# A region-attention and depthwise-convolution kernel: the convolution of image 2 in two halves, its steps and image 1's spread over bands 19 to 32, and the projection to 256 channels spread over three regions

## The chip, the cores and the metric

The kernel runs on one core of one Trainium2 chip. A core has five engines that run their own instruction streams in program order: TensorE (matmul, PE in the profile, with PEld for its weight loads), VectorE (DVE), ScalarE (ACT), GpSimdE (POOL) and SyncE (SP), which here only issues DMAs. The metric is the time of the device in microseconds, and the median of three runs stands for the kernel before.

## The reference

The input is four images of 128 channels and 128 x 128 pixels. The first layer takes from each image 9 x 9 overlapping regions of 16 x 16 pixels (step 14) and does in each a LayerNorm over channels, attention with four heads of 32, a projection and a residual; overlapping pixels are averaged. Then comes a LayerNorm over channels, a projection from 128 to 256 channels, a depthwise 5 x 5 convolution, a batch norm with the statistics of all four images, two GELUs, a projection back to 128 and a residual:

```
out = zeros.at[:, :, ih, iw].add(reg2);  merged = out / cnt
y  = ln(merged^T) @ w_p0 + b_p0                      # 128 -> 256 channels
ym = conv(ym, dw_k, padding 2, feature_group_count=256)   # depthwise 5x5
ym = batchnorm over (batch, rows, columns) of ym
y  = gelu(gelu(ym)) @ w_p2 + b_p2 + merged
```

The second layer quantises activations and weights and does two 3 x 3 convolutions with batch norms and a residual. The change doesn't touch it.

## The kernel before, in words

The first layer runs in 36 bands (`bands`, t = 0 to 35): band t is row i = t mod 9 of regions of image t // 9, with 9 regions side by side. All engines but POOL run in the order in which the program lists the work (`tc.manual_schedule`). The loop over t goes through the nine regions j of a band; for each it issues `scores(j)` (L784, with the exponentials L792 on ACT), then the pending `values` of the region before (L847, L855, and on DVE L867 to L871), and between these four lists of side work that `beside(t)` has planned for region j.

The side work of band t is the LayerNorm and the q/k projections of band t+1 (`ln1_chunks`, two blocks of rows a1 and a2), the output projection, second LayerNorm and projection to 256 of band t-1 (`post_chunks`, blocks b1 and b2), and steps of the depthwise convolution of rows that are complete. The last four entries of a block, b1[7:] and b2[7:], are its projection to 256, called `p0` (L561): four matmuls `pm<-xn,wp` (eight PE instructions, L438), one ACT instruction into a tile `y` (L567), and a store of that tile to the scratch tensor `y2_d`. There are four `y` tiles, two for each half of the 256 channels (L204), taken in turn. So a `p0` must wait until the store of the tile two before in its half has landed. In bands from 10 on, b1's four `p0` run in region 8 and b2's four in region 0 of the next band (`left`, L922); in bands up to 9 they are spread over three regions (L939).

The depthwise convolution is done on TensorE with band matrices. `units` (L170) lists its portions: images 0 to 2 each as a whole (8 groups of 16 rows), image 3 as 4, 2 and 2 groups. `conv_steps(n)` (L615) makes a portion's steps: the first only loads two tiles ahead, each of the rest loads the tile two ahead (`w<-dw_d` L587, `u<-y_d` L634) and does the `products` of one: matmuls L601 into two PSUM tiles `pm`, two ACT copies `c` (L648), bn_stats on DVE (L652) and stores of the copies to `cv_d`. A whole image has 32 such tiles of 2 x 4 channels by 8 groups (48 instructions on PE with 512 columns, four u loads, two w loads for every second tile, two stores of 256 KB). A half of an image has 16 tiles of 2 x 8 channels by 4 groups (96 instructions with 256 columns, four u loads, two w loads, four stores of 128 KB). The copies lie in the pool `cp`, two buffers each of c0 and c1, so four. There are three `pm` buffers in PSUM, which all side work shares, and three buffers each for u and w. The last portion, two groups, is done after the bands by `conv_rest` (L679, copies L721).

Stores are not issued where they arise: `run` (L944) issues on SP, after each piece of side work, the stores that were pending before it. SP has one queue in program order, and each DMA waits there for what it needs; the DMAs use eight semaphores in turn, and a new DMA on a semaphore waits until the one before it on the same semaphore is complete.

How many steps a band gets is set in `beside` by `todo` and `share`: a whole image's 33 steps are dealt over nine bands (3 or 4 a band: bands 10 to 18 and 19 to 27), image 2's over five (L893: 6 or 7 a band, bands 28 to 32), image 3's first half in bands 33 and 34 (8 and 9), its next portion in band 35 (17). Up to nine steps go to regions in the order of the tuple (1, 3, 5, 7, 8, 4, 6, 2, 0): four steps to regions 1, 3, 5, 7, a fifth to region 8, seven to 1, 3, 4, 5, 6, 7, 8. In odd regions a step is in the second list, in even ones at the end of the fourth.

After the bands come `conv_rest`, the batch norm's constants, `gelu_stage` and `last_stages`.

Of the kernel before, what the change touches and what calls it, by code (L numbers as in the profile page):

```python
# [8 lines left out]
F32 = mybir.dt.float32  # L9
# [5 lines left out]
P = 128  # L15
# [4 lines left out]
NR = (P - RS) // STEP + 1  # L20
# [11 lines left out]
GR = 16  # L32
CW = P // 2
KD = 2 * (GR + 4)
NCK = 8
# [11 lines left out]
def layers(  # L47
# [30 lines left out]
    B = x.shape[0]  # L78
# [45 lines left out]
    g1, b1 = vector(ln1_g, "g1"), vector(ln1_b, "b1")  # L124
# [3 lines left out]
    g2, b2 = vector(ln2_g, "g2"), vector(ln2_b, "b2")  # L128
# [7 lines left out]
    with (  # L136
# [21 lines left out]
        for w in (wqkv, wp0.rearrange("p h m -> p (h m)")):  # L158
            n = w.shape[1]
# [8 lines left out]
    bands = [(b, i) for b in range(B) for i in range(NR)]  # L168

    units = [(b, 0, P // GR) for b in range(B - 1)] + [(B - 1, g, n) for g, n in ((0, 4), (4, 2), (6, 2))]  # L170

# [13 lines left out]
    with ExitStack() as actx:  # L185
# [12 lines left out]
        pool = lambda name, bufs: bctx.enter_context(tc.tile_pool(name=f"{name}_{tag}", bufs=bufs))  # L198
        xp, yp, sums = pool("xp", 2), pool("yp", 2), pool("sums", 1)
        up, cp = pool("up", 3), pool("cp", 2)  # L200
        att, attn_t, attn_v = pool("att", 2 if safe else 4), pool("attn_t", 2), pool("attn_v", 2)
# [413 lines left out]
        def conv_steps(n, ahead=2):  # L615
# [6 lines left out]
            nj = nc_ // 4  # L622
# [18 lines left out]
            def products(at):  # L641
# [4 lines left out]
                for half in range(2):  # L646
                    cv = cp.tile([P, nj, ng, CW], F32, name=f"c{half}")
                    nc.scalar.copy(  # L648
# [30 lines left out]
        def conv_rest(n, w_t, u_t, c_t):  # L679
# [32 lines left out]
            def step(k):  # L712
# [168 lines left out]
        def beside(t, sel=None):  # L881
# [5 lines left out]
            two = post_chunks(t - 1, sel) if t else []  # L887
            had = len(todo)
            if t >= 2:
                b, i = bands[t - 2]  # L890
                if i == NR - 1 and b < B - 1:
                    todo.extend(conv_steps(b))
                    share[0] = NR if b < B - 2 else 5  # L893
                elif b == B - 1 and i == 4:
                    todo.extend(conv_steps(B - 1))
                    share[0] = 2
                elif b == B - 1 and i == 6:
                    todo.extend(conv_steps(B))
                    share[0] = 1

            fresh = len(todo) > had
            n = len(todo) // share[0] if fresh else -(-len(todo) // max(share[0], 1))
            conv = [todo.pop(0) for _ in range(n)]
            share[0] -= 1
            a1, a2 = one if one else ([None] * 9,) * 2
# [9 lines left out]
            d = [[] for _ in range(NR)]  # L915
            twice = len(conv) > NR
# [34 lines left out]
        T = len(bands)  # L951
        todo, share, left, early = [], [0], [], []
        wq, kscale = [], []
# [3 lines left out]
        todo += band_matrices()  # L957
        share[0] = NR + 1
        for blk in row_blocks(0):
# [447 lines left out]
```

## Time and profile before

| What | Value |
|---|---|
| median of 3 runs | 3240.15 us (3233.6 to 3244.1) |
| profiled execution | 3249.98 us, span 3248.2 us |
| PE busy | 3059.6 us, 94% of the span |
| DVE, ACT, POOL busy | 62%, 61%, 26% |
| DMA | 681.70 MB, mean 210 GB/s |
| bands 19 to 32 (1022.5 to 1913.9) | 891.4 us, PE 848.8 us busy, DMA share 0.86 |
| bands 33, 34, 35 | 82.6, 98.3, 104.8 us |

A band starts where its first exponential (L792) starts; there are 18 in each band. In the windows below, each line gives a stretch, its length, each engine's busy time with its instruction count, the granted clock of TensorE, the share of time that the 16 DMA engines were busy, and GB/s. The count on PE tells how many convolution steps a band had: a band without any has 736 (two records are missing in the one shown), each tile of a whole image adds 48, each tile of a half 96. Busy time of PE is modelled, so that a busy PE may be one that waits inside a matmul group.

### The profile page before, as it was taken

The numbers are of one execution on the slowest core, as the hardware profiler recorded it, in microseconds if no ns is written. First come the engines' busy times: TensorE is split into PE (matmuls) and PEld (weight loads), VectorE is DVE, ScalarE is ACT, GpSimd is POOL, SyncE is SP. The second block draws the span as 40 slices with busy tenths as digits, with TensorE's granted clock in tenths as the row PEclk, the third lists the DMA queues.
The fourth block names the chain that finished last, engine by engine and source line by source line (L and its number), as shares of the span: only waits on it lengthen the run. The fifth ranks groups of instructions, "written<-read, shape, count | busy, mean of one in ns | idle before, by whom it ended". The sixth has DMA issues, their size and how long they took to land.

```text
span 3248.2 us, 92154 instructions
## 1 busy us (share of the span) xinstructions
PE 3059.6 (94%) x39162; PEld 1480.1 (46%) x39162; DVE 2014.5 (62%) x3244; ACT 1988.5 (61%) x2658; POOL 840.9 (26%) x1058
## 2 busy tenths in 40 slices
PE   7999999999999999999888998876899999999998
PEld 4555544444444444444344444453544444444443
DVE  5777886766766777676555664542455555666543
ACT  5777777777776777677555655432477777433443
POOL 3444443333333333333222232211111111000000
PEclk9999999999999999999999998876799999999999
DMA  3555677888886888886898988857899999452398
GB/s 82 151 167 162 176 186 191 203 199 204 215 193 169 191 206 211 196 213 172 179 202 201 209 188 203 196 158 187 264 354 359 358 359 304 162 167 80 110 357 311
DMA packets 809891, 681.70 MB, mean 210 GB/s; under 512 B 580918, under 2 KB 695935, under 8 KB 809471
## 3 DMA queue, kind: packets, MB, share of 16 engines
q1 hardware_dynamic: 798879, 669.17, 75.8%
q8 instruction: 311, 5.10, 0.7%
q0 software_dynamic: 1024, 3.93, 0.5%
q10 hardware_dynamic: 9568, 2.61, 0.3%
q14 instruction: 109, 0.89, 0.1%
HBM read 408.72 MB, written 270.79 MB: 209 GB/s over the span
## 4 chain that ended last, share of the span: by engine, by line
PE 76%; DMA 9%; ACT 5%; issue 4%; SPq 3%; DVE 2%; ACTq 0%; POOL 0%; DVEq 0%; POOLq 0%
PE pc L1164 21%; PE pm L438 16%; PE sc L784 9%; PE pm L601 9%; PE po L847 8%; PE pb L1228 6%; PE po L855 3%; DMA y_d<-y 3%; PE pm L377 3%; ACT pt L792 2%; DMA u<-y_d 2%; DMA xn<-row 1%; SPq L451 1%; SPq L431 1%; ACT v L775 1%
## 5 line engine op out<-in xcount | busy, mean ns | idle before, releaser
L867 DVE RECIPROCAL rd<-po 128x256 f32<-128x256 f32 x324 | 568.8, 1756 | 439.1 <-PE po L855 438.5
L1164 PE MATMUL pc<-q,wq 128*128 128x512 fp8e4 x3168 | 700.3, 381 | 5.1 <-DVE q L1176 5.1
L792 ACT ACTIVATE pt<-sc 128x1024 f32<-128x1024 f32 x648 | 628.2, 1025 | 119.1 <-PE sc L784 63.2
L802 POOL TENSOR_TENSOR sm<-pt 128x512 f32<-128x512 f32 x324 | 415.7, 1283 | 1047.3 <-ACT pt L792 727.0
L1164 PEld LDWEIGHTS <-wq 128*128 128x128 fp8e4 x3168 | 309.0, 98 | 406.7 <-issue 38.9
L784 PE MATMUL sc<-q,kr 32*128 32x256 f32 x5184 | 413.6, 417 | 27.3 <-ACT pt L792 27.1
L601 PE MATMUL pm<-u,w 40*32 40x504 f32 (+5 forms) x7680 | 369.6, 503 | 41.7 <-DMA u<-y_d 29.7
L784 PEld LDWEIGHTS sc<-q,kr 32*128 32x128 f32 x5184 | 254.1, 191 | 286.4 <-issue 177.1
L847 PE MATMUL po<-pt,v 128*32 128x256 f32 x5184 | 364.9, 401 | 10.0 <-DVE part L871 6.9
L648 ACT COPY c<-pm 128x512 f32<-128x512 f32 (+1 forms) x256 | 132.4, 563 | 272.3 <-PE pm L601 243.3
L438 PE MATMUL pm<-xn,wp 128*32 128x512 f32 (+1 forms) x2304 | 248.1, 553 | 44.6 <-ACT y L567 42.6
L567 ACT ACTIVATE y<-pm,vectors 128x512 f32<-128x512 f32 (+1 forms) x288 | 183.1, 641 | 166.0 <-DMA y_d<-y 111.9
L802 DVE TENSOR_TENSOR sm<-pt 128x512 f32<-128x512 f32 x324 | 244.2, 754 | 35.8 <-ACT pt L792 35.8
L438 PE MATMUL pm<-xn,wqkv 128*32 128x512 f32 (+1 forms) x2304 | 245.3, 548 | 4.9 <-ACT v L775 3.5
L601 PEld LDWEIGHTS pm<-u,w 40*32 40x32 f32 x7680 | 147.6, 112 | 223.1 <-issue 153.0
L652 DVE BATCH_NORM_STATS2 st<-c 128x6 f32<-128x512 f32 (+2 forms) x320 | 160.9, 550 | 134.8 <-ACT c L648 134.3
L1228 PE MATMUL pb<-cv,wp 128*128 128x512 f32 x512 | 232.1, 596 | 4.9 <-ACT cv L1219 4.9
L847 PEld LDWEIGHTS po<-pt,v 128*32 128x32 f32 x5184 | 140.5, 112 | 186.5 <-issue 103.5
L1172 DVE BATCH_NORM_STATS2 st<-pc 128x6 f32<-128x512 f32 x256 | 165.7, 689 | 84.7 <-PE pc L1164 84.7
L855 PE MATMUL po<-sm,ones 128*32 128x256 f32 x2592 | 206.1, 389 | 0.0
L874 POOL TENSOR_TENSOR ob<-ob,part 128x32 f32<-128x32 f32 x288 | 127.2, 442 | 230.6 <-DVE part L871 224.8
L438 PE MATMUL pm<-wqkv,yr 128*32 128x128 f32 x5184 | 176.3, 273 | 1.2 <-issue 1.2
(157 smaller groups left out, 3394.2 us busy)
## 6 DMA issues: line engine op xcount, KB each, us to landing
cv<-cv_d SPq DMA_DIRECT2D x64, 1024.0 KB
u<-y_d SPq DMA_DIRECT2D x234, 256.0 KB
cv_d<-c SPq DMA_DIRECT2D x192, 256.0 KB
y_d<-y SPq DMA_DIRECT2D x160, 256.0 KB
xn<-row SPq DMA_DIRECT2D x76, 512.0 KB
xfl<-xf_d SPq DMA_DIRECT2D x64, 512.0 KB
id_d<-y SPq DMA_DIRECT2D x64, 512.0 KB
idt<-id_d SPq DMA_DIRECT2D x64, 512.0 KB
```

The source lines that it names most:

```text
L438: nc.tensor.matmul(out[m], w[:, m], v, start=True, stop=True)
L567: nc.scalar.activation(y[:, :n], pm[:, : n * P].rearrange("p (r c e) -> p r e c", r=n, e=2), AF.Identity, bias=bp0[:, h : h + 1],)
L601: nc.tensor.matmul(outs[half][32 * q : 32 * q + 32, j, :, a:z], wt[hs, s, c, :], ut[hs, :, c, a + s - 1 : z + s - 1], start=(s == 1), stop ...
L784: nc.tensor.matmul(sc[h // 2][:, h % 2, kc, :].rearrange("p (r c) -> p r c", c=RS), region(kr, j)[hs, kc * P : (kc + 1) * P], queries(j, h ...
L792: nc.scalar.activation(pt, sc[p], AF.Exp)
L802: add(sm, pt[:, :, 0, :], pt[:, :, 1, :], ALU.add)
L847: nc.tensor.matmul(po[hs, 0, :], v[:, kc, hs], pt[h // 2][:, h % 2, kc, :], start=(kc == 0), stop=(kc == 1),)
L855: nc.tensor.matmul(po[hs, 1, :], ones, sm[h // 2][:, h % 2, :], start=True, stop=True)
L867: nc.vector.reciprocal(rd, po[:, 1, :])
L1164: nc.tensor.matmul(pc[:, h], w[:, t, :], q1[b][:, r + dy : r + dy + RB, dx : dx + P], start=(t == 0), stop=(t == 8),)
L1172: nc.vector.bn_stats(st[:, 2 * n + h, :], pc[:, h])
L1228: nc.tensor.matmul(pb[:, m], wp2[:, h, :], cv[:, h, px], start=(h == 0), stop=(h == 1))
```

## The change

Image 2's convolution is listed in two portions of four groups (64 rows), as image 3's first is, so there are seven portions in place of six. A portion's steps are put on the list when the rows that it needs are complete, at the bands in `ready`. The number of steps in a band now follows one line: 33 over bands 10 to 18, then the 67 of image 1 and of both halves of image 2 over bands 19 to 32, which gives 4, 5, 5, 5, 4, 5, 5, 5, 5, 4, 5, 5, 5, 5. Bands 33 to 35 keep 8, 9 and 17.

In bands 10 to 31 the projection to 256 is split: b1's first two `p0` stay in region 8, its last two move to region 0 of the next band, where one of b2's follows, and b2's last three go to region 2. In a band at which a portion becomes ready all six that are left over stay in region 0.

The copies `c` share three buffers in place of four, in `conv_steps` and in `conv_rest`. The tile of statistics has seven entries per channel group in place of six.

```diff
-    units = [(b, 0, P // GR) for b in range(B - 1)] + [(B - 1, g, n) for g, n in ((0, 4), (4, 2), (6, 2))]
+    units = [(b, 0, P // GR) for b in range(B - 2)]
+    units += [(b, g, n) for b, g, n in ((B - 2, 0, 4), (B - 2, 4, 4), (B - 1, 0, 4), (B - 1, 4, 2), (B - 1, 6, 2))]
...
-        up, cp = pool("up", 3), pool("cp", 2)
+        up, cp = pool("up", 3), pool("cp", 3)
...
-                    cv = cp.tile([P, nj, ng, CW], F32, name=f"c{half}")
+                    cv = cp.tile([P, nj, ng, CW], F32, name="c")
...
-                    cv = c_t.tile([P, 4, ng, CW], F32, name=f"c{half}")
+                    cv = c_t.tile([P, 4, ng, CW], F32, name="c", bufs=3)
...
-                if i == NR - 1 and b < B - 1:
-                    todo.extend(conv_steps(b))
-                    share[0] = NR if b < B - 2 else 5
...
+                if (b, i) in ready:
+                    todo.extend(conv_steps(ready[b, i]))
+            last = T - NR + 6
+            if t <= NR:
+                n = -(-len(todo) // (NR + 1 - t))
+            elif t < last:
+                whole, at = 4 * NCK + 1, t - NR
+                due = whole * at // NR if at <= NR else whole + (2 * whole + 1) * (at - NR) // (last - 2 * NR - 1)
+                n = min(len(todo), due - taken[0])
+                taken[0] += n
+            else:
+                n = len(todo) // 2 if t == last else len(todo)
...
-                d[j] = [conv.pop(0)] if twice and j and conv else []
+                d[j] = [conv.pop(0)] if j and len(conv) > NR - 1 - j else []
...
-            f, left[:] = list(left), b2[7:]
+            apart = t + 1 < last
+            f, left[:] = list(left), [*(b1[9:] if apart else []), *b2[7:]]
+            g = len(f) if t >= 2 and bands[t - 2] in ready else 3
...
-                ([a1[1]], [], f, [*c[0], a1[2]]),
+                ([a1[1]], [], f[:g], [*c[0], a1[2]]),
...
-                ([a2[1]], [a1[4]], b1[:2], [*c[2], a2[2]]),
+                ([a2[1]], [a1[4]], [*f[g:], *b1[:2]], [*c[2], a2[2]]),
...
-                ([], [b2[6], x2], b1[7:], [*c[8], s1]),
+                ([], [b2[6], x2], b1[7 : 9 if apart else None], [*c[8], s1]),
...
+        ends = [(b, NR - 1) for b in range(B - 2)] + [(B - 2, 4), (B - 2, NR - 1), (B - 1, 4), (B - 1, 6)]
+        ready = {at: n for n, at in enumerate(ends)}
```

More of the change, by code (lines that the diff above doesn't have):

```diff
@@ L887, in beside @@
             two = post_chunks(t - 1, sel) if t else []
-            had = len(todo)
             if t >= 2:
                 b, i = bands[t - 2]
-                if i == NR - 1 and b < B - 1:
-                    todo.extend(conv_steps(b))
-                    share[0] = NR if b < B - 2 else 5
[L894 to L902, printed above, removed]
+                if (b, i) in ready:
[10 more added lines that the diff above has]
+                n = len(todo) // 2 if t == last else len(todo)
             conv = [todo.pop(0) for _ in range(n)]
-            share[0] -= 1
             a1, a2 = one if one else ([None] * 9,) * 2
@@ L915, in beside @@
             d = [[] for _ in range(NR)]
-            twice = len(conv) > NR
             for j in sorted((1, 3, 5, 7, 8, 4, 6, 2, 0)[: len(conv)]):
                 c[j] = [conv.pop(0)]
-                d[j] = [conv.pop(0)] if twice and j and conv else []
+                d[j] = [conv.pop(0)] if j and len(conv) > NR - 1 - j else []
             x1 = lambda: fetch(t, 0)
             x2 = lambda: fetch(t, 1)
-            f, left[:] = list(left), b2[7:]
+            apart = t + 1 < last
+            f, left[:] = list(left), [*(b1[9:] if apart else []), *b2[7:]]
+            g = len(f) if t >= 2 and bands[t - 2] in ready else 3
             s1 = early[0][0] if early else None
             plan = [
-                ([a1[1]], [], f, [*c[0], a1[2]]),
+                ([a1[1]], [], f[:g], [*c[0], a1[2]]),
                 ([], [a1[3], *c[1]], [], [a2[0]]),
-                ([a2[1]], [a1[4]], b1[:2], [*c[2], a2[2]]),
+                ([a2[1]], [a1[4]], [*f[g:], *b1[:2]], [*c[2], a2[2]]),
                 ([], [a2[3], *c[3]], [], [b1[2]]),
@@ L951, in layers @@
         T = len(bands)
-        todo, share, left, early = [], [0], [], []
+        todo, left, early, taken = [], [], [], [0]
+        ends = [(b, NR - 1) for b in range(B - 2)] + [(B - 2, 4), (B - 2, NR - 1), (B - 1, 4), (B - 1, 6)]
+        ready = {at: n for n, at in enumerate(ends)}
         wq, kscale = [], []
@@ L957, in layers @@
         todo += band_matrices()
-        share[0] = NR + 1
         for blk in row_blocks(0):
```

## The prediction

> **What bounds the kernel now.** I read the page first (PE is busy 94% of the span, so a gain must come from where PE waits or runs at half clock), then a table of bands, then the waits and the timeline where bands are long.
>
> ```profile
> PE 3059.6 (94%) x39162; PEld 1480.1 (46%) x39162; DVE 2014.5 (62%) x3244; ACT 1988.5 (61%) x2658; POOL 840.9 (26%) x1058
> PEclk9999999999999999999999998876799999999999
> ```
>
> Windows of bands 12, 14, 18, 28, 29, 35, and of the stretch of bands 19 to 32:
>
> ```profile
> 622.10:678.50 56.40, 56.25 (x928) 26.56 (x923) 40.69 (x63) 41.44 (x64) 21.18 (x27) 1.00 0.90 209
> 736.30:794.30 58.00, 56.17 (x928) 26.50 (x920) 40.69 (x63) 41.42 (x64) 21.17 (x27) 1.00 0.87 205
> 966.90:1022.50 55.60, 54.65 (x880) 26.03 (x872) 39.73 (x61) 40.84 (x63) 21.11 (x27) 1.00 0.63 163
> 1540.20:1608.60 68.40, 65.01 (x984) 29.71 (x976) 40.54 (x65) 43.47 (x67) 19.90 (x25) 0.95 0.80 173
> 1608.60:1688.00 79.40, 71.21 (x1072) 32.43 (x1068) 45.38 (x71) 44.74 (x71) 21.12 (x27) 0.94 0.92 201
> 2094.80:2199.60 104.80, 79.09 (x1960) 49.84 (x1957) 43.90 (x106) 37.43 (x66) 17.30 (x20) 0.79 0.63 166
> 1022.50:1913.90 891.40, 848.80 (x13280) 395.85 (x13272) 578.48 (x898) 591.73 (x899) 292.27 (x371) 0.97 0.86 197
> ```
>
> Four tiles (x928) take 56.4 to 58.0 us, three 55.6, seven (x1072) 79.4. So a tile costs some 1 to 2 us up to the fourth and over 7 us beyond it. The first of three reasons is in the timeline of ACT and PE at band 29:
>
> ```profile
> 1597.56 1.07 ACT L648 COPY c<-pm 128x512 f32<-128x512 f32 x2 [1.36 <-PE pm L601]
> 1606.65 1.07 ACT L648 COPY c<-pm 128x512 f32<-128x512 f32 x2 [2.00 <-PE pm L601]
> 1618.03 0.58 ACT L567 ACTIVATE y<-pm,vectors 128x384 f32<-128x384 f32 x1 [4.94 <-DMA y_d<-y]
> 1626.06 0.58 ACT L567 ACTIVATE y<-pm,vectors 128x384 f32<-128x384 f32 x1 [5.68 <-DMA y_d<-y]
> ...
> 1618.66 1.20 PE L438 MATMUL pm<-xn,wp 128*32 128x384 f32 x8 [4.02 <-ACT y L567]
> 1629.17 2.99 PE L784 MATMUL sc<-q,kr 32*128 32x256 f32 x16 [2.87 <-ACT pt L792]
> ```
>
> ACT stands in p0 until the y stores of region 8 land, and PE behind it. After such a stall the granted clock is 0.5 for 3.4 to 6.8 us. In bands 29 to 32 ACT waits 45.2 us for these stores (waits of 1608 to 1914), in bands 12 to 18 13.8. Second, the DMA engines: share 0.92 in band 29. Third, SP, from 28 on: the stores of the copies at 1597.56 are issued only at
>
> ```profile
> 1604.66 2.50 SPq L431 DMA_DIRECT2D cv_d<-c  x2
> 1607.21 4.91 SPq L451 DMA_DIRECT2D xr<-in_x_dram  x1
> 1612.21 4.55 SPq L431 DMA_DIRECT2D y_d<-y  x3
> ```
>
> **The change part by part.** The sum is made against the profiled execution, 3249.98 us, 9.8 (0.3%) above the median; 9.7 us is also about what a measurement can tell from no change.
>
> *Tiles on PE.* The unstalled groups cost the same in both forms, 48 instructions of 512 columns and 96 of 256:
>
> ```profile
> 1623.53 2.78 PE L601 MATMUL pm<-u,w 40*32 40x512 f32 x48
> ...
> 1976.42 2.89 PE L601 MATMUL pm<-u,w 40*32 40x256 f32 x96
> ```
>
> (others of x96 take 2.72 from start to the next instruction). So halving image 2 costs PE nothing; bounds 0 and 32 x 0.11 = 3.5 us. *TensorE: Matmul & The Clock Gate*, section "Wait — 56ns, not 53.3ns?", gives a fixed 2.5 ns for every matmul, which speaks against 1536 more instructions; by it the estimate would be 3.8 us more, where the row says 0 to 3.5.
>
> *DMAs of image 2.* A tile of a half issues ten DMAs (4 u, 2 w, 4 stores) for seven: 32 x 3 = 96 more on SP, at some 0.4 to 0.6 us each 40 to 58 us of SP, which in bands 20 to 26 issues for 24 to 34 of 57 us. The moved steps issue nothing on POOL or ACT, so SP is the only queue that they are moved past. Engine time, from the packets of the trace: u packets of 2048 B at 142 ns in band 34 (320 a tile, 45 us) for 1024 B at 79 ns (640, 51 us); w 120 packets more at 75 ns (9 us); stores of 256 B packets the same. Together +3 us over 16 engines is 0.25 a tile, 8 us for 32.
>
> *Bands 19 to 32.* Tiles per band become 3, 5, 5, 5, 4, 5, 5, 4, 5, 4, 4, 5, 5, 5 (begin steps at 19, 26, 29). Four tiles: 57.3, the mean of such bands. Five: band 28 had five in 68.4 us; 3.3 us of PE idle (waiting for u of the rows just stored, and exp) and half of 6.8 us at clock 0.5 belong to its begin, which leaves 61.7. Lower bound 56.4 + 2.8 = 59.2, if PE alone counts; upper 57.3 + (78.2 - 57.3) / 3 = 64.3, on the line to the seven-tile bands (mean of 29 to 31). I take 61.7, a band of just this load. Band 19: 60.2 and one tile, 61.7. Six p0 in region 0 at bands 24 and 28: +1.5 each (band 10 has six and waits 1.9 us for y). At 29 the begin step falls into region 7 and its first tile into region 8, some 6.5 us later, where SP needs 3.2 us to issue its six loads and u takes 6.3 to land: +6 with the half clock (2 to 10). Begin at 26: +1. Sum 9 x 61.7 + 4 x 57.3 + 61.7 + 3 + 6 + 1 = 856 for 891.4: **-35**. Cross-check by DMA: the share 0.855 of 891.4 is 762 us of engines, with 8 more 770; over 856 a share of 0.90. The highest share in any band is 0.92, which sets the floor at 837 (-54; the GELU stage, 2317 to 2690 us, reaches 0.99, so it is not a hard one); at the old share the stretch takes 900 (+9).
>
> What goes with a stall here: once y is on time, u and the c stores are late next, since DMA stays full. b1's xn is held one region longer; its buffer is wanted by a2's xn load in region 3, two regions later: nothing, and if p0 were that late, SP would stop at L411. DVE gets 64 more bn_stats (128 x 413 ns for 64 x 684: +9.1 us) where it is busy 45 of 79: nothing.
>
> *p0 split, bands 11 to 18.* Clean 56.2, mean of the four-tile bands 57.1; half a dozen such: **-5** (0 to -8).
>
> *Three c buffers.* The second copy of a tile now waits until the first store of the tile before has landed. With two regions between tiles, it would have had 0.4 us or more left in bands 11 to 26 (store landings by the semaphore records): nothing. From region 7 to 8 it has not: copies 9.1 us apart (the rows above), 1.8 less by two p0 fewer, 0.5 more for the second, against a landing 8.0 to 9.1 us after the first copy's end (0.5 later): a wait of 1 to 2 us on ACT. Behind it stand the squares L371 and the next band's exp; PE reaches the sum of squares 0.7 us after them. So some 0.8 us in nine bands: **+7** (0 to 14). In bands 33 and 34 tiles lie one region apart. There the second copies come 0.1 to 9 us too early, 60 us summed over 13; since a wait also puts the next tile later, about half, 30, stays. Most of it is SP being behind, and waiting longer for a store does not make SP later, since loads of u wait for products, not for copies: **+10** (0 to 30). In band 35, likewise 62 us, half 31; but SP issues 161 DMAs for 88.7 of 104.8 us, it sets the pace:
>
> ```profile
> 2137.75 4.83 SPq L431 DMA_DIRECT2D cv_d<-c  x8
> 2142.68 1.58 SPq L587 DMA_DIRECT2D w<-dw_d  x2
> 2144.30 1.57 SPq L634 DMA_DIRECT2D u<-y_d  x4
> 2145.97 3.03 SPq L431 DMA_DIRECT2D cv_d<-c  x4
> ```
>
> so **+4** (0 to 31). In `conv_rest` the second copies have 2.0 to 4.6 us left: 0. The aggregates (64 x 265 ns) grow by a sixth, the last eight are bare: +0.4. One p0 moved at band 34 and a shorter queue at 33: -1.
>
> Sum: -35 - 5 + 7 + 10 + 4 + 0.4 - 1 = -20, so 3230 on the profile's scale and **3220** by the median.
>
> **Rivals.** (A) Slower: the wait for the c stores passes in full to PE in bands 33 to 35, where exp is queued behind the copies and PSUM has three `pm`: 30 + 31 + 14 - 35 - 5 = +35, 3275. It turns the sign when more than 1.0 us of wait per tile reaches PE in these 32 tiles (35 + 5 - 7 = 33). For it: slots that already wait for stores (8.3 us, L648, in band 35). Against it: PE is idle 25.7 of 104.8 us there, mostly for u. (B) The DMA engines were the bound all along, and spreading keeps the share at some 0.875: the stretch takes 880, -11, and -5 + 21 leaves +5: no change, 3245. For it: 0.90 and 0.92 in 12 and 29. Against: band 18 with 0.63, band 28 with 0.80, room that spreading fills. (C) Better: five tiles cost what PE asks and the copies are covered: -54 - 5 + 3 = -56, 3184. For it: band 12 held 0.90 of DMA with PE idle 0.15 us. That the steps don't move can't be: the order is written out.
>
> **How the numbers follow.** Forecast 0.42 (range 3203 to 3234), C 0.2, B 0.19, A 0.19. Faster: 0.4 of the forecast's 0.42, and C: 0.60. Same: most of B and the rest: 0.19. Slower: A and a little of B: 0.21. The range leaves out the far ends of C and A: 3182 to 3262.
>
> **What would show it.** Right: bands 20 to 31 at 57 to 62 us with x928 and x976 (x1216 for five tiles of a half), ACT waiting under 20 us for y stores from band 11 to 32, clock 1.0 there but at 19 and 29; DMA share near 0.90. Wrong: ACT L648 waiting for cv_d stores over 20 us, bands 33 to 35 together over 310 us (285.7 before), five-tile bands at 64 or more.

## The result, and the profile after

The changed kernel takes 3257.8 us in the median of seven runs (3242.0 to 3263.1), where the kernel before takes 3238.7 beside it: ratio 1.005, 95% interval 1.003 to 1.0071. It is slower by half a per cent; the prediction said faster by 0.6%, to 3220. The profiled execution took 3261.4 us, 11.4 more than that of before, where the sum had -20. (Line numbers after the change are one higher than before: the copies are L649, the p0 matmuls L439, the projection's ACT instruction L568.)

The page of the changed kernel, busy times and granted clock, then the groups that the prediction spoke of:

```profile
PE 3064.1 (94%) x40698; PEld 1511.7 (46%) x40698; DVE 2023.7 (62%) x3308; ACT 1984.7 (61%) x2658; POOL 838.8 (26%) x1058
...
PEclk9999999999999999999998988977699999999999
...
L649 ACT COPY c<-pm 128x512 f32<-128x512 f32 (+1 forms) x256 | 135.2, 562 | 360.9 <-PE pm L602 241.7
...
L439 PE MATMUL pm<-xn,wp 128*32 128x512 f32 (+1 forms) x2304 | 256.7, 566 | 16.1 <-ACT y L568 9.0
...
L568 ACT ACTIVATE y<-pm,vectors 128x512 f32<-128x512 f32 (+1 forms) x288 | 182.7, 642 | 99.5 <-PE pm L439 55.6
```

The stalls that the change was priced by did go: PE's wait for `y` is 9.0 us, and the stores of `y` no longer head the list of what ACT waits for before a `y`. The time is elsewhere. Windows of the changed kernel: bands 20, 21, 22, 25 (five whole tiles each), 26 (four tiles of a half and a begin step), 29, 30, 31 (five tiles of a half in the last two), 35; then bands 19 to 25, 26 to 32, 19 to 32 and 33 to 35. (Start and end, length, busy time with count of PE, PEld, DVE, ACT, POOL, granted clock, share of the DMA engines, GB/s.)

```profile
1080.10:1146.80 66.70, 63.73 (x995) 29.49 (x984) 42.57 (x67) 42.44 (x66) 21.10 (x27) 0.95 0.87 196
1146.80:1209.40 62.60, 59.93 (x968) 27.33 (x968) 41.63 (x66) 42.47 (x66) 21.08 (x27) 1.00 0.93 207
1209.40:1273.50 64.10, 59.48 (x968) 27.49 (x968) 41.73 (x66) 42.45 (x66) 21.05 (x27) 0.99 0.93 206
...
1393.70:1452.20 58.50, 58.02 (x956) 26.89 (x960) 41.22 (x65) 42.14 (x66) 20.04 (x24) 1.00 0.94 216
1452.20:1521.80 69.60, 63.16 (x1132) 32.59 (x1124) 42.16 (x72) 42.63 (x65) 21.43 (x27) 0.95 0.80 188
1652.30:1719.60 67.30, 61.71 (x1112) 32.68 (x1104) 41.47 (x72) 41.51 (x65) 21.03 (x27) 0.93 0.77 184
1719.60:1789.30 69.70, 62.91 (x1240) 33.91 (x1234) 43.00 (x76) 42.41 (x65) 21.03 (x27) 0.97 0.79 191
1789.30:1859.20 69.90, 64.80 (x1208) 34.66 (x1208) 42.52 (x76) 42.42 (x66) 21.09 (x27) 0.93 0.82 197
2110.30:2217.50 107.20, 82.31 (x2056) 50.83 (x2048) 44.62 (x106) 37.64 (x67) 17.23 (x20) 0.79 0.66 175
1022.30:1452.20 429.90, 415.36 (x6645) 192.55 (x6640) 288.99 (x450) 294.47 (x450) 145.12 (x184) 0.98 0.90 205
1452.20:1929.30 477.10, 441.32 (x8168) 234.23 (x8160) 294.79 (x513) 297.89 (x453) 146.34 (x187) 0.94 0.82 196
1022.30:1929.30 907.00, 856.68 (x14805) 426.79 (x14796) 583.77 (x963) 592.35 (x902) 291.47 (x371) 0.96 0.86 200
...
1929.30:2217.50 288.20, 234.94 (x5052) 135.53 (x5052) 138.14 (x278) 128.01 (x209) 58.15 (x71) 0.87 0.76 184
```

Set against the sum of the prediction, on the scale of the two profiled executions:

| stretch | before | predicted | measured |
|---|---|---|---|
| bands 0 to 9 | 506.2 | 506.2 | 505.2 |
| bands 10 to 18 (first steps of the split) | 516.3 | 511.3 | 517.0 |
| bands 19 to 25: 32 whole tiles | 405.7 | 429.0 | 429.9 |
| bands 26 to 32: 32 tiles of a half | 485.7 | 427.2 | 477.1 |
| bands 33 to 35 | 285.7 | 299 | 288.2 |
| after band 35 | 1048.6 | 1049 | 1041.6 |

(The two rows in the middle are the prediction's band prices taken apart: 6 x 61.7 + 57.3 + 1.5, and 4 x 61.7 + 3 x 57.3 + 1.5 + 6 + 1. The 7 us of the prediction for waits between regions 7 and 8 are left out here; they lie in nine of the bands 19 to 32.) One row is wrong by 50 us. Of the others, bands 10 to 18 miss the forecast by 6 us, and bands 33 to 35 and the part after band 35 came out 11 and 7 us under it; these partly make up for the 50. Bands of five whole tiles cost what was said, 62.8 us in the mean against 61.7. Bands of five tiles of a half, 27 and 30 to 32, take 69.5. Yet their DMA engines have a share of 0.79 to 0.86, less than the 0.93 of the shorter bands 21 and 22: in the mean of the 16, the engines are less busy there, not more. PE's own work grew little; it waits more, in short pieces, and runs at 0.90 to 0.98 of its clock after them.

The other thing that stands out is what ACT and PE wait for. The view of waits of the changed kernel, ACT's copies and then PE (us in total, times, longest):

```profile
ACT c L649 <- DMA cv_d<-c: 113.4, 36, 7.2
...
PE pm L378 <- ACT sq L372: 48.4, 28, 5.1
PE pm L602 <- DMA u<-y_d: 25.6, 14, 5.9
PE sc L785 <- ACT pt L793: 17.7, 32, 2.1
PE pm L439 <- ACT y L568: 9.0, 2, 8.5
```

and the same of PE in the kernel before:

```profile
PE pm L438 <- ACT y L567: 42.6, 14, 13.6
PE pm L601 <- DMA u<-y_d: 29.7, 18, 6.3
...
PE pm L377 <- ACT sq L371: 7.1, 13, 2.0
```

What PE waited for `y`, it now waits for the squares `sq`, which stand on ACT behind a copy that waits for a buffer. The timeline of band 30 shows one such place:

```profile
1782.63 0.58 ACT L649 COPY c<-pm 128x512 f32<-128x512 f32 x1 [2.02 <-PE pm L602]
...
1787.88 0.58 ACT L649 COPY c<-pm 128x512 f32<-128x512 f32 x1 [4.66 <-DMA cv_d<-c]
1788.36 1.06 ACT L372 ACTIVATE sq<-xt 128x1024 f32<-128x1024 f32 x1
...
1789.47 1.08 PE L378 MATMUL pm<-sq,ones 128*32 128x256 f32 x8 [2.53 <-ACT sq L372]
```

That is the chain of rival A, and it would have been easy to stop here and blame the third buffer. The first experiments ask whether it is the cause.

### The profile page after: what moved, and what is told of

It reads as the page before. It is cut to its first block, busy times and chain, and to the rows that moved or that the text cites. A ratio compares the mean times of both kernels' runs of the same rounds, so it can differ in the third digit from the quotient of the medians.

```text
span 3259.1 us, 95441 instructions
## 1 busy us (share of the span) xinstructions
PE 3064.1 (94%) x40698; PEld 1511.7 (46%) x40698; DVE 2023.7 (62%) x3308; ACT 1984.7 (61%) x2658; POOL 838.8 (26%) x1058
## 3 DMA queue, kind: packets, MB, share of 16 engines
q0 software_dynamic: 1024, 3.93, 0.4%
## 4 chain that ended last, share of the span: by engine, by line
PE 74%; DMA 11%; ACT 5%; issue 4%; DVE 3%; SPq 3%; ACTq 0%; POOL 0%; DVEq 0%; POOLq 0%
PE pc L1165 21%; PE pm L439 16%; PE sc L785 8%; PE pm L602 8%; PE po L848 8%; PE pb L1229 7%; PE po L856 3%; PE pm L378 3%; DMA cv_d<-c 3%; ACT pt L793 2%; DMA u<-y_d 2%; DMA row<-rstd 2%; DMA y_d<-y 1%; DMA xr<-in_x_dram 1%; DVE rd L868 1%
## 5 line engine op out<-in xcount | busy, mean ns | idle before, releaser
L793 ACT ACTIVATE pt<-sc 128x1024 f32<-128x1024 f32 x648 | 627.9, 1024 | 125.0 <-PE sc L785 70.9
L785 PE MATMUL sc<-q,kr 32*128 32x256 f32 x5184 | 405.1, 411 | 20.9 <-ACT pt L793 17.7
L602 PE MATMUL pm<-u,w 40*32 40x252 f32 (+5 forms) x9216 | 367.6, 444 | 39.9 <-DMA u<-y_d 25.6
L649 ACT COPY c<-pm 128x512 f32<-128x512 f32 (+1 forms) x256 | 135.2, 562 | 360.9 <-PE pm L602 241.7
L653 DVE BATCH_NORM_STATS2 st<-c 128x6 f32<-128x256 f32 (+2 forms) x384 | 167.6, 484 | 217.9 <-ACT c L649 217.6
L439 PE MATMUL pm<-xn,wp 128*32 128x512 f32 (+1 forms) x2304 | 256.7, 566 | 16.1 <-ACT y L568 9.0
L602 PEld LDWEIGHTS pm<-u,w 40*32 40x32 f32 x9216 | 173.4, 110 | 207.7 <-issue 129.7
L439 PE MATMUL pm<-xn,wqkv 128*32 128x512 f32 (+1 forms) x2304 | 246.8, 551 | 6.3 <-ACT v L776 4.4
L568 ACT ACTIVATE y<-pm,vectors 128x512 f32<-128x512 f32 (+1 forms) x288 | 182.7, 642 | 99.5 <-PE pm L439 55.6
L439 PE MATMUL pm<-wqkv,yr 128*32 128x128 f32 x5184 | 184.8, 283 | 0.0
```

Of the source, the lines that this page charges most:

```text
L439: nc.tensor.matmul(out[m], w[:, m], v, start=True, stop=True)
L568: nc.scalar.activation(y[:, :n], pm[:, : n * P].rearrange("p (r c e) -> p r e c", r=n, e=2), AF.Identity, bias=bp0[:, h : h + 1],)
L602: nc.tensor.matmul(outs[half][32 * q : 32 * q + 32, j, :, a:z], wt[hs, s, c, :], ut[hs, :, c, a + s - 1 : z + s - 1], start=(s == 1), stop ...
L653: nc.vector.bn_stats(st0[:, k, half, 2 * jj + c0 // 4 + j, n, :], cv[:, j].rearrange("p g x -> p (g x)"))
L785: nc.tensor.matmul(sc[h // 2][:, h % 2, kc, :].rearrange("p (r c) -> p r c", c=RS), region(kr, j)[hs, kc * P : (kc + 1) * P], queries(j, h ...
L793: nc.scalar.activation(pt, sc[p], AF.Exp)
```

## Experiments on the waits for copies

Each kernel ran beside the kernel before on the same chip, which took 3251.5, 3239.1, 3250.6 and 3252.2 us beside the four sets of runs below. So across sets ratios are compared; they are to the kernel before, with 95% intervals. First the changed kernel with four copy buffers. To make room, the statistics of the last portion are put into a small tile late, after band 35 (estimated at about 3 us).

```diff
-        up, cp = pool("up", 3), pool("cp", 3)
+        up, cp = pool("up", 3), pool("cp", 4)
...
-                    cv = c_t.tile([P, 4, ng, CW], F32, name="c", bufs=3)
+                    cv = c_t.tile([P, 4, ng, CW], F32, name="c", bufs=4)
```

> The changed kernel with four c buffers in place of three; the statistics of the last portion lie in a small tile of conv_rest, so that the fourth buffer finds room. Theory W (the copies wait for the stores of the tile before): ACT's waits for cv_d stores fall from 113 us to under 20, bands 19 to 32 from 907 to 855-875 us, bands 33 to 35 from 288 to 280-288, and the median to 3200-3220. Theory H (tiles of a half cost more by themselves, by ten DMAs on SP in place of seven): bands 26 to 32 stay at 465-477 us and the median at 3240-3260. Theory S (the DMA engines are full, whatever the buffers): bands 19 to 32 stay at 890-907 us with a DMA share that does not rise over 0.87.

Measured: 3287.1 us, ratio 1.012 (1.0104 to 1.0137). The waits for copies are all but gone, and the kernel is slower than the changed one. The view of waits of this kernel:

```profile
ACT y L568 <- DMA y_d<-y: 88.6, 43, 16.2
...
ACT c L649 <- DMA cv_d<-c: 10.7, 4, 3.7
```

The waits for stores of `y`, 38.5 us in the changed kernel, are back at 88.6. Its bands 19 to 25 took 430.0 us and 26 to 32 488.6, so bands 19 to 32 and the total are above what any of the three theories had given. Of the 20 us between the two profiled executions 11 lie after band 35 (1053.0 us, where the changed kernel took 1041.6 and the kernel before 1048.6). So that a fourth buffer makes the bands slower is not shown; that it does not cure them is.

The counterpart: the kernel before with three copy buffers and nothing else.

```diff
-        up, cp = pool("up", 3), pool("cp", 2)
+        up, cp = pool("up", 3), pool("cp", 3)
...
-                    cv = cp.tile([P, nj, ng, CW], F32, name=f"c{half}")
+                    cv = cp.tile([P, nj, ng, CW], F32, name="c")
```

> The kernel before with three c buffers, nothing else changed. Theory W: ACT waits 60-120 us for cv_d stores, most of it in bands 28 to 35 where tiles lie one region apart; the median is 20-45 us above the kernel before. Theories H and S: within 10 us of the kernel before.

Measured: 3244.6 us, ratio 0.9979 (0.9965 to 0.9993), a little faster than with four. The view of waits of this kernel, ACT and PE:

```profile
ACT c L648 <- DMA cv_d<-c: 117.3, 41, 7.0
...
ACT y L567 <- DMA y_d<-y: 65.9, 55, 8.5
...
PE pm L377 <- ACT sq L371: 41.1, 24, 6.0
...
PE pm L438 <- ACT y L567: 17.9, 11, 7.4
PE pm L601 <- DMA u<-y_d: 13.6, 9, 3.6
```

ACT waits as long for copies here as in the changed kernel, PE nearly as long for `sq` (41.1 us, there 48.4), and the kernel is not slower, where theory W had wanted 20 to 45 us more: PE's waits for `y` and for `u` fall by as much (42.6 and 29.7 to 17.9 and 13.6). The two runs agree from both sides: having three buffers in place of four moves waits from `y` and `u` to `c`, and it doesn't lengthen the kernel.

## Experiments on the parts of the change

The projection split alone, in the kernel before:

```diff
-                ([a1[1]], [], f, [*c[0], a1[2]]),
+                ([a1[1]], [], f[:g], [*c[0], a1[2]]),
...
-                ([a2[1]], [a1[4]], b1[:2], [*c[2], a2[2]]),
+                ([a2[1]], [a1[4]], [*f[g:], *b1[:2]], [*c[2], a2[2]]),
```

> The kernel before with the projection to 256 spread over three regions in bands 10 to 31, nothing else changed. If y stores hold ACT in the kernel before: ACT's wait for y stores falls from 112 to 30-60 us, bands 29 to 32 from 305 to 285-297 us, and the median by 10-25 us. If other waits take their place: within 8 us of the kernel before.

Measured: 3233.0 us, ratio 0.9947 (0.9929 to 0.9965), a gain of 17 us, within the forecast. Where it arises is another matter. Bands 10 to 18 took 510.5 us (-6) and 19 to 25 396.0 (-10), but bands 29 to 32, which were to fall to 285 to 297 us, took 307.0 (305.4 before), and ACT still waits 66.5 us for stores of `y`, over the 30 to 60 expected. So this part of the change gains, but not in the bands from whose stalls the gain was argued.

The other part alone: image 2 in halves, dealt over bands 28 to 32 as before, four copy buffers (and the late statistics):

```diff
-                    todo.extend(conv_steps(b))
+                    todo.extend(conv_steps(b) if b < B - 2 else conv_steps(b) + conv_steps(b + 1))
```

> The kernel before with image 2 in two halves, dealt over the same bands 28 to 32, with four c buffers (the statistics of the last portion in a small tile of conv_rest). Theory H: bands 28 to 32 grow from 374 to 400-425 us and the median by 25-50 us. Theory W: bands 28 to 32 stay within 10 us of 374, the median within 12 us of the kernel before.

Measured: 3276.0 us, ratio 1.0088 (1.0071 to 1.0105). Bands 28 to 32 went from 373.7 to 393.6 us, between the ranges of the two theories; some 4 us more lie after band 35, with the late statistics. The halves alone lose what the whole change loses and more. So the next question was what in the form of a half tile costs.

## Experiments on the price of a half tile

Against a whole tile, a tile of a half has matmuls of 256 columns, four stores instead of two, and its own load of `w`, where two whole tiles share one. Each was put by itself on the whole tiles of the kernel before. Matmuls of images 0 to 2 in two runs of 256 columns:

```diff
-            for j in range(n // 4):
+            ng = ut.shape[1]
+            for j, g in [(j, g) for j in range(n // 4) for g in range(0, ng, 4)]:
+                gs = slice(g, min(g + 4, ng))
```

> The kernel before with the convolution matmuls of images 0 to 2 done in two runs of 256 columns in place of one of 512, as in the tiles of a half; loads, copies and stores as before. Theory P (the 96 smaller matmuls of a half's tile make it dearer inside a band, although an unstalled group takes the same 2.7 us): 0.6 to 1.5 us for each of 96 tiles, the median 50-140 us above the kernel before. Theories D and B: within 10 us.

Measured: 3245.8 us, ratio 1.0029 (1.0011 to 1.0046), 6.7 us in the median for 96 tiles, 0.07 a tile, inside the bounds 0 to 0.11 of the prediction. That is 1.5 ns for each of 4608 more instructions. By the 2.5 ns that the Trainium skill, *TensorE: Matmul & The Clock Gate*, section "Wait — 56ns, not 53.3ns?", gives for a matmul at the full clock, an estimate would be 11.5 us, which the interval (3.6 to 14.9) does not exclude.

The copies of whole images stored by two DMAs of 128 KB each:

```diff
-                        store(
-                            bass.AP(
+                        for g in range(0, ng, 4):
+                            m = min(4, ng - g)
+                            store(
+                                bass.AP(
```

> The kernel before with each copy of images 0 to 2 stored by two DMAs of 128 KB in place of one of 256 KB: the same bytes in the same 256-byte pieces, two DMAs more per tile, 192 in all. Theory D (the number of DMAs sets the pace, by SP's issue time and by eight in flight): 0.4 to 1 us per tile, 35-95 us above the kernel before. Theories P and B: within 10 us.

Measured: 3241.8 us, ratio 1.0006 (0.9991 to 1.0021). Twice the number of stores costs nothing that could be measured, so the number of DMAs by itself (theory D) is not what is dear.

`w` loaded for every tile:

```diff
-                if c == 0:
-                    W[k, jj] = up.tile([P, 3, 8, 32], F32, name="w")
-                    weights(W[k, jj], k, jj, 1, nc.sync.dma_start)
+                W[k, jj] = up.tile([P, 3, 8, 32], F32, name="w")
+                weights(W[k, jj], k, jj, 1, nc.sync.dma_start)
+                V[at] = W[k, jj]
```

> The kernel before with w loaded for every tile of images 0 to 2 and not for every second, as in the tiles of a half: one DMA of 120 KB more per tile, 96 in all, 11.5 MB. Theory B (the bytes of w on a full set of DMA engines): 0.5 to 1.2 us per tile, 50-115 us above the kernel before. Theory D: a third of what st2's two more DMAs cost, and more by half. Theory P: within 10 us.

Measured: 3276.7 us, ratio 1.0103 (1.0061 to 1.0145): 37 us for 48 more loads of 240 KB (two DMAs of 120 KB each), 0.8 us each. That is less than theory B had given for their bytes (50 to 115 us), but here is a price that the prediction didn't have.

And a probe in the other direction, fewer DMAs for a tile: each half of `u` in one DMA of 40 partitions, where it was one of 32 and one of 8.

```diff
-                    for a, z in ((0, GR), (GR, GR + 4)):
+                    for a, z in ((0, GR + 4),):
                         nc.sync.dma_start(
                             out=ut[64 * half + 2 * a : 64 * half + 2 * z]
```

> The kernel before with each half of a u tile loaded by one DMA of 40 partitions in place of one of 32 and one of 8, in all steps of images 0 to 3: two DMAs less per tile, the same bytes and pieces. Theory D: 35-95 us below the kernel before. Theories P and B: within 10 us.

Measured: 3196.9 us, ratio 0.9877 (0.9849 to 0.9904), 42 us less. Bands 28 to 32 went from 373.7 to 358.7. The windows of bands 21 to 23, twelve tiles each, of the kernel before and then of this one:

```profile
1138.80:1310.70 171.90, 169.65 (x2768) 80.03 (x2760) 121.90 (x189) 124.10 (x191) 63.43 (x81) 1.00 0.88 205
```

```profile
1127.20:1296.90 169.70, 168.74 (x2768) 79.79 (x2760) 121.99 (x189) 124.24 (x191) 63.34 (x81) 1.00 0.77 209
```

The same tiles and GB/s, but the DMA engines' share is 0.77 for 0.88. In the trace's list of the DMA engines' packets, those of 1024 B, which are those of `u` and `w`, take 55 ns in the mean in these bands where they took 79. SP was not relieved: over bands 19 to 32 its DMA instructions sum to 525.0 us, 485.7 before, though there are 570 of them for 697, as the stores of copies behind the joined loads take longer to issue (200.8 us for 96.1). So the gain is not shown to come from fewer entries in SP's queue; it goes with the shorter packets.

## The half tile in the place of a whole one

The bands with half tiles differ from the others in place too: the begin steps at 26 and 29 and rows just written. To separate form and place, image 1 of the changed kernel was put in halves as well, by turns, so that bands 19 to 25 have the same number of tiles at the same places and no begin step more. (Statistics late, as above.)

```diff
-            tiles = [(k, jj, c) for k in range(NCK) for jj in range(2) for c in range(0, 8, nc_)]
+            tiles = [
+                (k, jj, c, n)
+                for k in range(NCK) for jj in range(2) for c in range(0, 8, nc_) for n in several
+            ]
...
-        ready = {at: n for n, at in enumerate(ends)}
+        ready = dict(zip(ends, [(0,), (1, 2), (3,), (4,), (5,), (6,)]))
```

> The changed kernel with image 1 in halves too: its 32 tiles are dealt as before (3, 5, 5, 5, 4, 5, 5 in bands 19 to 25), the two halves by turns, each tile with its own load of w; all rows of image 1 are long there, and there is one begin step. (The statistics of the last portion are taken late, as in the run with four c buffers, some 3 us after band 35.) In the changed kernel bands 19 to 25 took 429.9 us with whole tiles (a five-tile band 62.8 in the mean), and five-tile bands of halves, 27 and 30 to 32, 69.5. Theory F (the form of a half tile is dear wherever five of it lie in a band): five bands go from 62.8 to about 69.5, so bands 19 to 25 take some 463 us. Theory L (the place is dear: bands 26 to 32 with two begin steps, rows just written, half clock after their stalls): only the extra matmuls (0.1 us a tile) and 16 more loads of w (37 us for 48 in the run that loaded w twice: 12 us) are added: at most 445 us. 455 tells them apart.

Measured: 3291.1 us, ratio 1.0134 (1.009 to 1.0178). And the same with one load of `w` for the two halves:

```diff
-                if c == 0:
+                if c == 0 and n == several[0]:
```

> As the run with image 1 in halves, but the two halves of a tile share one load of w, so there is no more w traffic than with whole tiles. If w is what makes a half tile dear, bands 19 to 25 come back to some 430 to 435 us. Theory F without w (matmuls of 256 columns, u in packets of 2048 B, stores of 4 groups): they stay at 455 or more. Theory L: 430 to 435 as well, but coming from at most 445.

Measured: 3271.7 us, ratio 1.0064 (1.0038 to 1.009). The windows of both: two bands of five tiles, then bands 19 to 25 and 26 to 32. Image 1 in halves:

```profile
1142.20:1212.50 70.30, 66.13 (x1208) 35.31 (x1208) 42.38 (x76) 42.78 (x67) 21.09 (x27) 0.90 0.84 197
1212.50:1279.60 67.10, 60.55 (x1208) 32.59 (x1208) 42.56 (x76) 41.96 (x67) 21.16 (x27) 1.00 0.85 203
...
1015.00:1476.80 461.80, 427.31 (x8184) 229.90 (x8176) 291.99 (x514) 294.14 (x450) 145.61 (x184) 0.96 0.84 200
1476.80:1946.50 469.70, 435.70 (x8192) 230.15 (x8188) 293.45 (x514) 297.23 (x453) 146.51 (x187) 0.96 0.82 198
```

With `w` shared:

```profile
1147.10:1213.30 66.20, 62.96 (x1208) 33.66 (x1208) 42.40 (x76) 42.68 (x66) 21.11 (x27) 0.95 0.84 196
1342.80:1405.00 62.20, 60.48 (x1221) 33.23 (x1210) 42.67 (x76) 42.42 (x67) 21.14 (x27) 1.00 0.86 205
1024.10:1464.30 440.20, 421.88 (x8184) 227.16 (x8180) 293.20 (x514) 294.94 (x451) 145.20 (x184) 0.98 0.86 200
1464.30:1944.30 480.00, 442.15 (x8192) 232.97 (x8188) 293.48 (x514) 297.20 (x452) 147.04 (x187) 0.94 0.82 193
```

With whole tiles bands 19 to 25 took 429.9 us (and 430.0 in the run with four copy buffers, the same code there). With halves they take 461.8, what the theory of the form expected (463); with `w` shared 440.2, between the two ranges expected (430 to 435, and 455 or more). So 32 us of form, of which some 22 go with 16 doubled loads of `w`, 1.4 us each; the medians of the two runs differ by 19. (The two profiled executions differ by 3 us only, as with `w` shared bands 10 to 18 and 26 to 32 happened to take 6 and 10 us more.) The 10 us of form that are left have no cause shown. In the second band shown, at full clock, PE is busy 60.55 us with five tiles of a half, against 59.93 with five whole ones in band 21: the work on PE is indeed the same. What is longer is the waiting, and the half clock after it, as in the first band shown (0.90, PE "busy" 66.13).

How sure is a single profile of a stretch? Bands 26 to 32 have the same code in the changed kernel, in the one with four buffers (apart from these) and in the two here, and took 477.1, 488.6, 469.7 and 480.0; bands 10 to 18 of the same four took 517.0, 509.3, 510.2 and 516.5. So such a stretch varies by some 4 to 10 us to either side, and a smaller difference between two profiles says nothing by itself.

If joining the loads of `u` shortens the bands with halves too, the changed kernel gains more from the joined load of `u` than the kernel before did; and the part of the change that works should add to it.

> The changed kernel with each half of u loaded by one DMA of 40 partitions, not of 32 and 8. In the kernel before that took 40 us (3239 to 3197; bands 28 to 32 fell by 15, 33 to 35 by 20). Theory D (bands with five half tiles are long because of the DMAs: SP's issues and the engines' time): bands 26 to 32 fall from 477 to about 435 and the total by 60 or more, to 3195 or less. Theory L (begin steps and the stalls and half clock behind them, not the amount of DMA): bands 26 to 32 stay above 460, and the total falls by 30 to 40, to about 3220.

> The kernel before with the projection to 256 spread over three regions and u in one DMA of 40 partitions: the two edits that made it faster. If they add up: 3239 - 40 - 17 = 3182 us. If both gain by making the same y stores land in time, the second has little left: 3192.

Measured: 3198.4 us, ratio 0.9838 (0.9804 to 0.9872), and 3195.5 us, ratio 0.9835 (0.98 to 0.987). The first takes 2.1% off the changed kernel (1.005 to 0.9838), where the same edit took 1.2% off the kernel before. Its bands 30 to 32, then 19 to 25 and 26 to 32:

```profile
1692.20:1754.40 62.20, 61.76 (x1240) 33.57 (x1232) 42.70 (x76) 42.60 (x66) 21.14 (x27) 0.98 0.78 205
1754.40:1817.70 63.30, 59.09 (x1208) 32.35 (x1208) 42.46 (x76) 42.32 (x66) 21.14 (x27) 1.00 0.83 218
1817.70:1879.10 61.40, 61.09 (x1212) 33.50 (x1216) 42.20 (x75) 43.78 (x68) 21.13 (x27) 0.97 0.86 222
1017.40:1433.70 416.30, 408.29 (x6648) 190.50 (x6640) 289.25 (x450) 294.21 (x450) 145.34 (x184) 1.00 0.84 213
1433.70:1879.10 445.40, 423.89 (x8192) 228.39 (x8188) 294.26 (x514) 297.20 (x452) 146.78 (x187) 0.97 0.79 208
```

Bands of five half tiles now take 61.4 to 63.6 us (63.6 is band 27, not shown), near the price that the prediction had given them. What is left above the prediction's 427 for bands 26 to 32 lies mostly in the two bands with a begin step, 26 (63.0 us for 58.3) and 29 (71.5 for 63.3). Bands 26 to 32 at 445 lie between the two theories' figures, nearer to that of the DMAs (435) than to that of the place (over 460), and the total, 3198 against 3195 or 3220, is that of the DMAs. The second run fits that the two edits that gain add up (0.9877 x 0.9947 is 0.9825), but its interval also holds 0.9855, which is what was expected if they do not. The rest of the change shows no worth beside them: 0.9838 with it, 0.9835 without, each known to some 0.0035.

## SP's queue or the DMA engines?

A load of `w` keeps SP for 0.77 us in the median of its 192 DMAs, and a tile of a half has two. Moving them to POOL's queue leaves the bytes as they are and takes them off SP. It changes their packets too: in the list of packets, the 192 loads are 5760 packets of 4096 B on POOL's queue, where they were 23040 of 1024 B on SP's. (Theory Q is that SP's queue is the limit, theory E the time of the DMA engines.)

```diff
-                    weights(W[k, jj], k, jj, 1, nc.sync.dma_start)
+                    weights(W[k, jj], k, jj, 1, nc.gpsimd.dma_start)
```

> As the run with image 1 in halves and a load of w for every tile, but all loads of w of the steps are issued on POOL's queue, not on SP's: the same DMAs and bytes, two instructions fewer on SP for every load. In that run bands 19 to 25 took 461.8 us; with w shared by the two halves 440.1. Theory Q (SP's queue: the loads of w stand ahead of u and of the stores there): the stretch falls to 445 or less. Theory E (the time of the DMA engines): it stays at 455 or more. A third case: POOL, in whose queue the loads now stand and wait for their buffers, holds up the sums of the softmax, and the stretch grows.

> The changed kernel with the loads of w issued on POOL's queue. Theory Q: bands 26 to 32 (477 us) fall by some 20, bands 33 to 35 by a few us, where SP issues most; the total to 3235 or less. Theory E: the total stays within 8 us of 3258.

> The changed kernel with u in one DMA of 40 partitions and the loads of w on POOL's queue. Theory Q: u1 has taken four DMAs a tile's pair off SP already; another 5 to 15 us fall, from 3198 to some 3188. Theory E: no change, 3198.

> The kernel before with the projection to 256 spread, u in one DMA of 40 partitions, and the loads of w on POOL's queue. Theory Q: 3195 falls by 5 to 10. Theory E: no change. Whether the change itself is worth anything once the DMAs are fewer is read from this run against the one before it.

Measured, in that order: 3254.5 us, ratio 1.0008 (0.9995 to 1.0021); 3229.0, 0.9911 (0.9878 to 0.9944); 3179.4, 0.9768 (0.975 to 0.9786); 3182.5, 0.9781 (0.9741 to 0.9822). In total the queue theory is met: the changed kernel goes from 1.005 to 0.9911. By place it is met in part. Windows of the changed kernel with `w` on POOL's queue, bands 19 to 25, 26 to 32, 33 to 35; then, of the kernel with image 1 in halves, bands 19 to 25:

```profile
1024.80:1453.50 428.70, 413.51 (x6645) 192.83 (x6640) 290.55 (x450) 293.95 (x450) 166.92 (x216) 0.99 0.95 205
1453.50:1915.80 462.30, 435.04 (x8192) 231.09 (x8188) 293.94 (x513) 297.44 (x452) 189.19 (x251) 0.96 0.87 202
1915.80:2188.30 272.50, 229.35 (x4948) 132.61 (x4948) 138.27 (x278) 128.18 (x208) 96.51 (x129) 0.87 0.86 192
```

```profile
1021.90:1483.20 461.30, 432.04 (x8180) 232.90 (x8176) 293.29 (x514) 295.39 (x451) 188.15 (x248) 0.95 0.89 199
```

Bands 33 to 35, where SP issues most, fall from 288.2 to 272.5, and 26 to 32 from 477 to 462, but bands 19 to 25 with image 1 in halves stay at 461, where the theory of the queue wanted 445 or less. The loads are not quite the same there: the share of the DMA engines rises from 0.84 to 0.89 at the same GB/s, and POOL stands some 121 us of the whole kernel in waits for a free `w` buffer. The engines' time for `w` did not fall by the move, neither in bands 33 to 35 (457 us summed over the packets, then 471) nor in bands 19 to 25 of the kernel with image 1 in halves (475, then 541), so the gain is not one of their engine time. But SP's time is no sure measure either: with `u` joined bands 33 to 35 of the changed kernel fall as far, to 270.8 us, and bands 26 to 32 by 32 us, while SP's DMA instructions take 205 us in the first (203 before) and 340 in the second (260 before).

So the doubled loads of `w` are shown as a cause. That they cost through SP's queue fits bands 33 to 35 and is not shown there; through what they cost in bands 19 to 32 stays open. The engines' share, lower in the slow bands than in the quick ones, speaks against their busy time in the mean; it is a mean over 16 engines, and as no record here says on which engine a packet ran, a few engines that are full among others that idle are not excluded.

With `u` joined and `w` on POOL's queue the kernel runs at 0.977 of the kernel before, the best of all, and again no difference can be seen whether the change's halves and dealing are in it (0.9768) or only its split projection (0.9781).

## Why the prediction was wrong

The step that failed is "61.7, a band of just this load", carried from five whole tiles to five tiles of a half. It predicted 427 us for bands 26 to 32, and they took 477. Of the 50 us, 31 lie in the four bands of five tiles (69.5 for 61.7 us each), 15 in the two with a begin step, 26 (69.6 for 58.3) and 29 (67.3 for 63.3), and the rest in band 28. The runs show parts of about the same size: the form, 32 us on image 1's 32 tiles, two thirds of it from loading `w` twice as often; and some 18 that are left for place, of which the begin step in band 26 shows most plainly (a band of four half tiles without begin took 61.2 in the kernel with image 1 in halves). The second part is a difference of single profiles, no more certain than 10 us, and its cause was not tested.

Behind that step stands the sentence on the DMAs of image 2. It counted what a tile of a half adds, ten DMAs for seven and 40 to 58 us of SP's time, and then charged only the engine time, 8 us over 32 tiles, and that as hidden. SP's time was over-priced: over bands 19 to 32 SP's DMA instructions took 502.3 us for 485.7 before, 17 more for 100 more DMAs. The stores indeed cost nothing, but a load of `w` cost 0.8 us in one setting and 1.4 in the other. There was a warning in the trace: the prediction's own band of four tiles of 0.90 DMA share ran PE without idle time, so share alone could not tell when a band turns long.

Point by point:

- The split projection, -5 in bands 11 to 18: right in direction by the run of it alone, which gains 17 us, 6 of them in bands 10 to 18 and 10 in bands 19 to 25, where the sum priced it only through its figures for whole bands. In the changed kernel itself bands 10 to 18 show no gain (517.0 us for 516.3). The mean of 57.1 from which the -5 was worked out takes in band 18, which has three tiles; bands 11 to 17 alone have 57.3, which changes the term by 1 us. ACT's waits for `y` stores fell from 111.9 to 38.5 us.
- Five whole tiles, 61.7: right. Bands 19 to 25 took 429.9 for 429.0. Six more tiles than before cost 24 us there, 4 each, as the sum had it.
- Halving costs PE nothing, 0 to 0.11 us a tile: right (0.07, with an interval of 0.04 to 0.16; 60.55 against 59.93 us a band).
- Three copy buffers, +7 +10 +4: the waits came, 113.4 us, over the 20 that the prediction had named as a sign of error. In the kernel before the same waits cost nothing in the total. Bands 33 to 35 grew by 2.5 us, not 13.
- Rival A saw the right chain, from the copy to `sq` to PE, at 48 us of PE's waiting, and its 3275 lies nearer to the measured 3258 than the forecast does. That is luck, as the reason was wrong: the kernel before with three buffers has the same waits and is not slower, and four buffers don't cure the change.
- Rival B, that the DMA side sets the pace all along, was nearest in kind and in time (3245): the stretch of bands 19 to 32 has a share of 0.86 before and after, and joining the loads of `u` and moving those of `w` both gained in the total. Yet twice the stores cost nothing, so it is not the DMA side as a whole. It put the stretch at 880, which took 907, as it too left out the price of more loads.
- Rival C, five tiles at what PE asks and covered copies, fell with the same step; with `u` joined, which is another kernel, bands 30 to 32 came to within 2 us of the forecast's own price.
- The range 3182 to 3262 holds 3257.8, at its far end.

## What to carry to other kernels

When work is recut into smaller pieces, count what each piece must load again, and price that by a run of the old kernel with just those loads doubled, not by the engine time of their bytes. A wait that appears in the profile at a new place is not a loss until one run without it, and one old kernel with it, say so: waits behind a shared resource move from one name to the next. Before spreading work over time to relieve a queue, try whether its loads can be joined; here that was worth more than all the rescheduling, though the number of entries is not what made it so, as doubling the stores cost nothing.

## What was not expected

One DMA of 40 partitions in place of one of 32 and one of 8 took 42 us off the kernel, and lowered the mean time of a 1024 B packet in bands 21 to 23 from 79 to 55 ns at the same bytes. The Trainium skill, *DMA: Bandwidth & Descriptors*, section "Why a DMA increments its semaphore by 16 and not by 1", says that a DMA is shared among the largest number of engines, up to 16, that divides the slowest dimension of both of its sides. By it the DMA of 40 would use ten engines, and those of 32 and 8 sixteen and eight, which does not explain a gain. The lists of packets agree with the rule in number: beside the data they hold packets of 4 B, on SP's queue 40070 in the kernel before and 36486 with `u` joined, 3584 fewer or 14 for each of the 256 joined loads, which is 16 + 8 less 10. They do not say which engines these were. Why the packets got shorter is open.

Taking 4608 matmuls of 512 columns into twice as many of 256 cost 1.5 ns each, and twice the number of stores at the same bytes nothing that could be measured (1.0006, 0.9991 to 1.0021), while 96 more loads of 120 KB cost 37 us.
